# Two weight-sum steps and one transpose step reordered at the entry of a four-layer graph network's last layer

## The chip, the core and the metric

The kernel runs on one core of one Trainium2 chip. The metric is device time in microseconds (us), from the start to the end of one execution. PE is the matrix engine, DVE the vector engine, ACT the scalar engine, POOL the general engine (GpSimd), and SP the engine that issues nearly all transfers here.[...]

## What is computed

The input `x` is 128 graphs of 64 nodes with 256 features; `adj` is a 64 by 64 adjacency matrix. Four graph layers follow each other, each inside a residual connection and a layer norm:

```
x = _layernorm(x + _L0_gnn_ref(x, adj, ...))
x = _layernorm(x + _L1_gnn_ref(x, ..., adj, ...))
x = _layernorm(x + _L2_gnn_ref(x, adj, ...))
x = _layernorm(x + _L3_gnn_ref(x, adj, ...))
```

Only the passage into the last layer matters here:

```
h = relu(einsum('ts,bsh->bth', adj, x @ Wg0 + bg0))
h = relu(einsum('ts,bsh->bth', adj, h @ Wg1 + bg1))
for p in range(1, MAX_SKIP + 1):          # window lengths 1, 2, 3, 4
    wins = windows of p neighbouring rows of h
    last = last hidden state of an LSTM of length p over each window
    h = h with the last row of each window set to last
```

So the third layer's output is normed, goes through two graph convolutions, and then through four LSTMs with window lengths 1 to 4, each with its own input weights `Wih[p-1]` and recurrent weights `Whh[p-1]`.

## The kernel before

**Blocks.** The last layer works on 16 blocks of 8 graphs (512 rows). A block's way from the third layer's result to the LSTM's input is one generator, `gcn`. Its steps are: scale (ACT, L1294; of the first four blocks, which are still on the chip); two norm steps, each of which transposes half of the block on PE (L1312), adds the residual rows `x2r` (DVE, L1318), takes the statistics (DVE, L95 to L98), raises the variance to the power -1/2 (POOL, L86), scales (POOL, L100) and writes the half to DRAM (SP, L1323); the first sum over neighbours (PE, L1280) with its copy `hT` (DVE L1343, ACT L1344); the two halves of the first weights (PE L1350, DVE L1352, ACT L1354); the two halves of the second (PE L1362, DVE L1365); and the second sum over neighbours with the write of `H` (PE L1280, DVE L1373, ACT L1374). The residual rows come from DRAM by `load_x2` (SP, L1004); those of blocks 0 and 1 are fetched long before, those of block 2 when its generator is first called. PE's results go into banks called `g` (two) and `l` (six).

**LSTMs.** The generator `lstm` handles a pair of groups (four blocks). It starts once blocks 0 and 1 are through. Many of its products are formed by seven multiplications in place of eight, from sums and differences of the four parts of a weight matrix. These weight sums are made once, on POOL: `first_sums` (L1397, four operations 128x384) for the windows of length 1, and `Weights.sums` (L1229, four operations 128x512) twice for each of the lengths 2 to 4, once for the input weights (`wx`) and once for the recurrent ones (`wh`). Each is also written to DRAM, for later pairs: L1399 (0.75 MB), and L1232 (2 MB for `wx`, 1.75 MB for `wh`). `prepare` is the generator that loads a length's raw weights (L1218, 1 MB each), and then makes and writes one set of sums at each later call. The sums on the data, `column_sums`, are L1417 to L1420, also on POOL.

**Order.** `given(do)` ties the instructions that it records behind the ones recorded before, on PE, DVE, ACT and POOL, so on these engines the order is that of the program's text. SP's is not tied: it follows from the scheduler of the language. At the entry a list of block numbers says which block makes its next step, and `side` says which steps are put between the LSTM's units (`put(0, first[0], 3, 4)` puts the length-2 sums after units 3 and 4).

Before the change the entry is: `first_sums`, then the list of steps, then the LSTM's beginning, then a few more steps, then the length-2 loads.

Of the kernel before, what the change touches and what calls it, by code (L numbers as in the profile page):

```python
# [41 lines left out]
def kernel(ctx: ExitStack, tc: tile.TileContext, i, out):  # L42
# [67 lines left out]
    def given(do, *args, **more):  # L110
        traced = nc.cur_bb.bb.instructions
        first = len(traced)
        with ExitStack() as order:
            for e in latest.values():
                order.enter_context(tc.issue_after(e))
            r = do(*args, **more)  # L116
        for t in traced[first:]:
            if t.engine in (mybir.EngineType.PE, mybir.EngineType.DVE, mybir.EngineType.Activation,
                            mybir.EngineType.Pool):
                latest[t.engine] = t  # L120
        return r
# [8 lines left out]
    with ExitStack() as two:  # L130
# [630 lines left out]
        def hidden(q, m):  # L761
            return Z[q][:, m, :] if m < 2 else Aq(q)[:, (m - 2) * QT:(m - 1) * QT]
# [15 lines left out]
        def put(q, m, p_):  # L778
            nc.scalar.activation(hidden(q, m), p_, AF.Identity, bias=b1[:, m:m + 1])
            nc.vector.bn_stats(st1[:, m, q, :], hidden(q, m))  # L780
# [300 lines left out]
        def prepare(q):  # L1081
            terms[q] = []
            later = [(k, n) for k in range(M1) for n in range(2)]

            def one():
                k, n = later.pop(0)
                given(relu, q + 2 + n, k)
            for g in range(2):
                b = lambda k, n, g=g: hidden(q + n, 2 * g + k)
                a = lambda m, k, g=g: w2[:, 2 * g + k, m * P:(m + 1) * P]  # L1090
                T = sums_in_order(b)
                next(T)
                one()
                yield
                terms[q].append((a, [SW[1][:, n, g] for n in range(4)], b, next(T)))
                one()
                if g == 0:
                    one()
                yield
            one()  # L1100
            yield
            one()
            one()
# [792 lines left out]
    parts = [gcn(n // 2, n % 2, gbank if n % 2 == 0 else lbank, "hT" if n % 2 == 0 else "xs") for n in range(4)]  # L1896
    first = [prepare(weights_of[0, p]) for p in (2, 3)]
    for p in (2, 3):
        weights_of[0, p].room()
    given(first_sums)  # L1900
    for n in [0, 0, 0, 1, 1, 0, 1, 0, 0, 1, 2, 0, 0, 2, 1, 2, 1, 0, 3, 1, 1, 1]:
        given(next, parts[n])
    lstms = [lstm(k) for k in range(NP)]
    next(lstms[0])
    for n in [2, 3, 2, 3, 2]:
        given(next, parts[n])
    next(first[0])

# [7 lines left out]
    for u, order in enumerate([(3, 2, 2, 3, 3), (3, 3, 2, 3)]):  # L1918
        for n in order:
            put(0, parts[n], u)  # L1920
    put(0, first[0], 3, 4)
    put(0, first[1], 8, 13, 15)

    def gap(u):
# [80 lines left out]
```

## Time and profile before

| What | Value |
|---|---|
| Median of 3 runs | 2040.4 us (2037.68 to 2045.28) |
| Profiled execution: its time, and its span | 2039.12 us, 2037.3 us |
| PE busy | 1940.1 us, 95% of the span |
| DVE, ACT, POOL busy | 1248.0, 988.0, 880.0 us |
| PE's share of the chain that ended last | 73% |
| PE busy in 750 to 760 us | 7.13 of 10 us |
| PE busy in 830 to 840 and 850 to 860 us | 8.57 and 7.87 of 10 us |
| SP waiting for L1229 before L1232, 755 to 870 us | 5.6 us (`wx`), 8.3 us (`wh`) |

The span is what the trace covers; the execution's own time is 1.8 us more. The last layer begins near 760 us and fills the rest. In a timeline line the columns are: start, duration, engine, source line, operation, output and inputs, shape, count, and in brackets the engine's idle time before it with what ended it. A line with x2 or x4 merges that many instructions; its duration goes from the first's start to the last's end. SPq is SP issuing a transfer: the duration is that of the issue, not of the transfer. `A` is the block's room on the chip, `x_dram` a DRAM tensor, and `sums` the DRAM copies of weight sums.

### The profile page before, as it was taken

What the parts mean: (1) busy time and instruction counts of PE and PEld (TensorE: products, weight loads), DVE (VectorE), ACT (ScalarE), POOL (GpSimd) and SP (SyncE); (2) the same over time, 40 slices, a digit from 0 to 9 for tenths busy, and PEclk for the clock granted to TensorE, in tenths of its full rate; (3) what the DMA queues carried; (4) which work ended last, traced back from release to release, by engine and by line L of the source; (5) the groups of instructions that cost most, each with busy time, mean ns of one, the idle gap of its engine ahead of it and who ended that gap; (6) DMA issues with size and microseconds to landing.
All of it is one profiled execution on the core that took longest, in us unless ns stands there. A gap on an engine that the chain in (4) does not pass through costs nothing.

```text
span 2037.3 us, 31496 instructions
## 1 busy us (share of the span) xinstructions
PE 1940.1 (95%) x11447; PEld 1337.8 (66%) x11447; DVE 1248.0 (61%) x2763; ACT 988.0 (48%) x1892; POOL 880.0 (43%) x1017
## 2 busy tenths in 40 slices
PE   5999999999999999899999999999999999999996
PEld 4667777766554445477678577667577668578685
DVE  7456565565456555765557865557775557664566
ACT  2766666666345633644343644333544333543333
POOL 1123333333445544564645543435543445444264
PEclk8999999999999998999999999999999999999999
DMA  5344443332302025433243243133143032132022
GB/s 129 85 67 65 83 68 55 66 45 39 51 22 60 38 93 185 148 139 107 86 162 92 66 155 136 39 132 88 58 152 121 24 111 66 47 119 78 0 62 73
DMA packets 236539, 173.84 MB, mean 85 GB/s; under 512 B 150624, under 2 KB 213600, under 8 KB 233056
## 3 DMA queue, kind: packets, MB, share of 16 engines
q1 hardware_dynamic: 234528, 169.86, 29.5%
q8 instruction: 90, 1.47, 0.3%
q0 software_dynamic: 1024, 1.05, 0.2%
q10 hardware_dynamic: 832, 0.92, 0.1%
q14 instruction: 65, 0.53, 0.1%
HBM read 110.18 MB, written 61.60 MB: 84 GB/s over the span
## 4 chain that ended last, share of the span: by engine, by line
PE 73%; DVE 14%; ACT 5%; DMA 3%; issue 3%; POOL 2%; SPq 1%; DVEq 0%; POOLq 0%; ACTq 0%
PE l L1728 27%; PE l L1684 8%; PE pz L845 4%; PE l L1463 4%; PE m L253 3%; PE pz L774 3%; PE m L324 3%; PE e L352 2%; PE m L446 2%; PE g L1362 2%; PE m L327 2%; PE z L361 2%; PE g L1350 2%; PE pz L1043 2%; DVE cell L1642 1%
## 5 line engine op out<-in xcount | busy, mean ns | idle before, releaser
L1728 PE MATMUL l<-hs,wh 128*128 128x256 f32 (+1 forms) x896 | 276.0, 399 | 3.7 <-DVE hs L1592 3.1
L1728 PE MATMUL l<-xs,wx 128*128 128x256 f32 (+1 forms) x896 | 276.2, 399 | 2.9 <-DVE gate L1747 2.7
L1743 ACT ACTIVATE kept<-l 128x256 f32<-128x256 f32 (+1 forms) x224 | 88.8, 403 | 333.2 <-PE l L1728 331.8
L86 POOL TENSOR_TENSOR ln_rs<-ln_rs,mhalf 128x2 f32<-128x2 f32 (+2 forms) x98 | 85.5, 873 | 367.4 <-DVE ln_rs L98 366.9
L1728 PE MATMUL l<-H,wx 128*128 128x256 f32 (+1 forms) x672 | 210.5, 402 | 4.3 <-DVE gate L1756 3.4
L1728 PE MATMUL l<-hid,wh 128*128 128x256 f32 (+1 forms) x672 | 208.7, 399 | 0.0
L1728 PEld LDWEIGHTS l<-hs,wh 128*128 128x128 f32 x896 | 169.1, 190 | 47.1 <-DVE hs L1592 5.7
L1728 PEld LDWEIGHTS l<-xs,wx 128*128 128x128 f32 x896 | 168.9, 190 | 46.1 <-issue 2.8
L1761 ACT ACTIVATE gate<-gate,bias 128x512 f32<-128x512 f32 (+1 forms) x280 | 170.6, 657 | 40.7 <-DVE gate L1752 34.8
L1684 PE MATMUL l<-H,wx 128*128 128x256 f32 (+5 forms) x672 | 185.2, 431 | 4.9 <-DVE H L116 2.7
L363 ACT ACTIVATE u<-z 128x1024 f32<-128x1024 f32 x128 | 130.3, 1026 | 68.8 <-PE z L361 67.7
L1684 PEld LDWEIGHTS l<-H,wx 128*128 128x128 f32 x672 | 118.8, 190 | 65.5 <-issue 34.2
L1728 PEld LDWEIGHTS l<-H,wx 128*128 128x128 f32 x672 | 125.7, 190 | 42.6 <-DVE gate L1756 7.4
L1728 PEld LDWEIGHTS l<-hid,wh 128*128 128x128 f32 x672 | 127.2, 190 | 32.0 <-issue 2.9
L1751 POOL TENSOR_TENSOR gate<-gate,kept 128x256 f32<-128x256 f32 (+1 forms) x84 | 65.1, 775 | 144.9 <-DVE kept L1749 136.2
L335 DVE TENSOR_TENSOR qs<-m,qs 64x256 fp32r<-64x256 f32 x128 | 54.0, 422 | 106.3 <-ACT qs L334 104.4
L361 PE MATMUL z<-gath_r,qs 128*128 128x512 f32 x256 | 100.4, 480 | 9.3 <-ACT u L363 8.9
L1756 DVE TENSOR_TENSOR gate<-l,gate 128x256 f32<-128x256 f32 (+1 forms) x112 | 50.0, 446 | 88.4 <-POOL gate L1751 64.3
L1596 POOL TENSOR_TENSOR hs<-hid 128x256 f32<-128x256 f32 (+1 forms) x28 | 26.0, 929 | 170.1 <-DVE hid L1628 87.0
L1650 ACT ACTIVATE gate<-cell 128x512 f32<-128x512 f32 (+1 forms) x88 | 58.6, 666 | 83.6 <-DVE cell L1642 61.5
L1638 POOL TENSOR_TENSOR cell<-gate,cell 128x512 f32<-128x512 f32 (+1 forms) x56 | 75.4, 1367 | 28.4 <-ACT gate L1761 28.4
L1745 DVE TENSOR_TENSOR gate<-l,kept 128x256 f32<-128x256 f32 (+1 forms) x112 | 49.1, 438 | 59.7 <-ACT gate L1761 32.6
(380 smaller groups left out, 4097.6 us busy)
## 6 DMA issues: line engine op xcount, KB each, us to landing
wx<-sums SPq DMA_DIRECT2D x9, 2048.0 KB
wh<-sums SPq DMA_DIRECT2D x9, 1792.0 KB
way<-st SPq DMA_DIRECT2D x54, 256.0 KB
st<-way SPq DMA_DIRECT2D x216, 64.0 KB
xin<-in_x SPq DMA_DIRECT2D x16, 512.0 KB
ld<-table SPq DMA_DIRECT2D x16, 512.0 KB
x_dram<-y SPq DMA_DIRECT2D x16, 512.0 KB
x2r<-x_dram SPq DMA_DIRECT2D x32, 256.0 KB
```

The costliest lines, as they stand in the source:

```text
L86: nc.gpsimd.tensor_tensor(dst, dst, mhalf[:, :n], OP.pow)
L253: nc.tensor.matmul(p_, xT[:, k, c * P:(c + 1) * P], w0[:, k, :], start=k == 0, stop=k == KD - 1)
L361: nc.tensor.matmul(z[:, k, :], L1[q]["qs"][c][:, s, k * P:(k + 1) * P], gath_r, start=True, stop=True)
L363: nc.scalar.activation(u, z, AF.Relu)
L845: nc.tensor.matmul(self.bank[at], lhs, rhs, start=first and n == 0, stop=n == len(self.terms) - 1, skip_group_check=True)
L1463: nc.tensor.matmul(self.bank[at], lhs, rhs, start=new, stop=True, skip_group_check=True)
L1638: nc.gpsimd.tensor_tensor(c, t, c, OP.mult)
L1684: nc.tensor.matmul(b, w.raw[0][:, k, at, m, :], x, start=k == 0, stop=k == KD - 1)
L1728: nc.tensor.matmul(self.banks[j], lhs, rhs, start=src == 0, stop=src == 1)
L1743: nc.scalar.activation(self.keep(j), b, AF.Copy)
L1751: e.tensor_tensor(t[0][:, 1], t[0][:, 1], k[5], OP.add)
L1761: given(lambda: nc.scalar.activation(dst, dst, f, bias=b))
```

## The change

In the entry, `first_sums` moves from ahead of all steps to behind the norm steps of blocks 0 and 1 and block 0's first sum over neighbours. The second norm step of block 1 (its transposes on PE, its addition on DVE, its power and scaling on POOL) moves ahead of block 0's first sum over neighbours. The length-2 raw weights are loaded first of all, and the length-2 sums, with their writes to DRAM, move into the entry: those of `wx` ahead of block 2's first step, and those of `wh` after block 2's second norm step. Their former places, behind units 3 and 4 of the LSTM, go. No operation is added or dropped.

```diff
@@
     first = [prepare(weights_of[0, p]) for p in (2, 3)]
     for p in (2, 3):
         weights_of[0, p].room()
-    given(first_sums)
-    for n in [0, 0, 0, 1, 1, 0, 1, 0, 0, 1, 2, 0, 0, 2, 1, 2, 1, 0, 3, 1, 1, 1]:
-        given(next, parts[n])
+    next(first[0])
+    order = [0, 0, 0, 1, 1, 1, 0, first_sums, 0, 0, 1, first[0], 2, 0, 0, 2, 1, 2, first[0], 1, 0, 3, 1, 1, 1]
+    for n in order:
+        if n is first_sums:
+            given(n)
+        else:
+            given(next, parts[n] if isinstance(n, int) else n)
     lstms = [lstm(k) for k in range(NP)]
     next(lstms[0])
     for n in [2, 3, 2, 3, 2]:
         given(next, parts[n])
-    next(first[0])
@@
     for u, order in enumerate([(3, 2, 2, 3, 3), (3, 3, 2, 3)]):
         for n in order:
             put(0, parts[n], u)
-    put(0, first[0], 3, 4)
     put(0, first[1], 8, 13, 15)
```

As built, the order on the engines changes in this way. PE: block 1's last four transposes (L1312) come ahead of block 0's L1280. DVE: block 1's second L1318 and its statistics come ahead of block 0's L1343. POOL: the four norms of blocks 0 and 1, then L1397, then L1229 on `wx`, then block 2's two norms, then L1229 on `wh`, then L1417. SP: the two loads L1218, the eight writes L1323, L1399, L1232 for `wx`, then L1004 for blocks 2 and 3, two loads of later blocks (L1298), four L1323, L1004, and L1232 for `wh`. Before, SP had L1004 for blocks 2 and 3 directly after the first eight L1323, and both L1232 some 60 us later.

## The prediction

> **What bounds the kernel now.** I read the page first: PE is busy 95% of the span, 31,496 instructions, and the chain that ended last is mostly matmuls, so time can only be won where PE stands still or runs slowly. The change touches 757 to 866 us, so the rest comes from there. The windows of that stretch (columns: total, PE, PE weight load, DVE, ACT, POOL busy, then clock, DMA share, GB/s) show where PE is not full:
>
> ```profile
> 760.00:770.00 10.00, 5.47 (x78) 4.51 (x78) 6.59 (x25) 3.06 (x6) 8.09 (x11) 0.54 0.67 248
> 770.00:780.00 10.00, 10.00 (x96) 6.04 (x89) 5.21 (x12) 4.06 (x8) 2.94 (x6) 0.78 0.52 158
> 780.00:790.00 10.00, 9.65 (x99) 6.49 (x98) 7.26 (x20) 4.03 (x8) 3.59 (x6) 1.00 0.58 203
> 840.00:850.00 10.00, 8.22 (x20) 3.53 (x19) 7.86 (x15) 6.20 (x10) 7.47 (x7) 1.00 0.58 238
> ```
>
> Two places stand out: the entry into the last layer (PE half idle at half clock), and 840 to 850. The timeline of the entry says why:
>
> ```profile
> 761.54 1.96 POOL L1397 TENSOR_TENSOR wh<-wih 128x384 f32<-128x384 f32 x2 [1.98 <-PE g L1312]
> 763.44 0.17 DVE L85 TENSOR_SCALAR ln_rs<-ln_mv 128x2 f32<-128x2 f32 x1
> ...
> 764.66 0.99 POOL L1397 TENSOR_TENSOR wh<-wih,wh 128x384 f32<-128x384 f32 x1
> ...
> 765.61 0.71 POOL L86 TENSOR_TENSOR ln_rs<-ln_rs,mhalf 128x2 f32<-128x2 f32 x1
> ...
> 767.03 1.25 PE L1280 MATMUL g<-bdT,A 64*64 64x64 f32 x32 [3.47 <-POOL A L100]
> ...
> 770.20 0.69 DVE L1343 COPY hT<-g 128x512 f32<-128x512 f32 x1 [2.59 <-PE g L1280]
> ...
> 775.55 1.85 SPq L1004 DMA_DIRECT2D x2r<-x_dram  x4
> ...
> 781.79 0.68 DVE L1318 TENSOR_TENSOR x2r<-g,x2r 128x512 f32<-128x512 f32 x1
> ```
>
> The first norm is ready for POOL at 763.61 (763.44 + 0.17), but POOL works on `first_sums` until 765.65: 2.0 us in which the norm waits and PE behind it. The last two lines are the ones to remember: SP fetches block 2's residual rows `x2r` at 775.55, DVE uses them at 781.79. That is 6.2 us of lead, and nothing waits.
>
> For the second place, DVE and PE, and then SP's queue further on:
>
> ```profile
> 836.11 3.29 DVE L116 TENSOR_TENSOR H<-gate,cell 128x512 f32<-128x512 f32 x2
> 840.79 1.29 DVE L116 TENSOR_TENSOR H<-gate,wh 128x512 f32<-128x512 f32 x2 [0.20 <-ACT gate L116]
> ```
>
> ```profile
> 842.83 1.10 PE L1463 MATMUL l<-wx,wih 128*128 128x512 f32 x2 [1.78 <-DVE hs L116]
> 851.61 1.13 PE L1463 MATMUL l<-wx,wh 128*128 128x512 f32 x2 [0.81 <-DVE gate L116]
> ```
>
> ```profile
> 826.82 0.32 SPq L1265 DMA_DIRECT2D way<-st  x1
> 828.86 1.74 SPq L1267 DMA_DIRECT2D st<-way  x4
> ...
> 979.63 0.34 SPq L1232 DMA_DIRECT2D sums<-wx  x1
> 980.07 0.38 SPq L1265 DMA_DIRECT2D way<-st  x1
> 987.12 1.75 SPq L1267 DMA_DIRECT2D st<-way  x4
> ```
>
> The same pair of multiplications takes 3.29 us while POOL runs the length-2 sums (L1229, 834.66 to 840.53) and 1.29 us after them. And a 256 KB transfer (`way`) whose reader follows at once is read 2.04 us after its issue when alone (826.82 to 828.86), but 7.05 us after it when a 2 MB write of sums stands 0.44 us ahead of it on the queue (980.07 to 987.12). That last figure decides my forecast.
>
> [...] here `way`, whose input DVE had ready at 835.60 (834.89 + 0.71), was issued at 840.99, just after the sums' write at 840.56. [...] Before, PE ends at 757.1, the clock is 0.50 from 761, and 1.00 again from 774.5, after near-unbroken work since 767.03.
>
> **The change part by part.** The base is the profiled execution: span 2037.3, its run 2039.12, 1.3 below the median 2040.4.
>
> 1. *first_sums behind the four norms of blocks 0 and 1.* POOL starts the first norm at 763.65 and not 765.61, 1.96 earlier. The next bound is DVE: block 1's second norm now stands ahead of block 0's `hT` copy. DVE's norms start at 761.71, 763.59 and 765.66, 1.95 each; four end at about 769.6. So `hT` is copied at 769.6 and not 770.20: 0.6 won of 1.96, by itself.
>
> 2. *Block 1's second transposes earlier.* Four transposes (1.11 us, half clock) leave 770.08 and go into the gap of 763.5 to 767. They lie beside the hT wait, so they add nothing to the 0.6.
>
> 3. *The POOL queue.* Four norms at 1.87 (765.61 to 767.48) bounded by DVE's 1.95: the last power starts at 763.65 + 3 x 1.95 = 769.5 and its scaling ends at 771.4. Then `first_sums`, 4.1 us (761.54 to 765.65), to 775.5. Then the length-2 `wx` sums, four of 1.27 plus gaps, 5.2 us (5.65 and 5.87 before, beside two-input DVE work that is absent here), to 780.7.
>
> 4. *The SP queue, the part that costs.* The program's SP order is now: `wx` and `wh` loads, eight `x_dram` writes, the write of first_sums (0.75 MB), the write of the `wx` sums (2 MB), and only then block 2's `x2r`. The 2 MB write waits for POOL at 780.7; `x2r` is issued 0.44 later, at 781.2, in place of 775.55, behind 2 MB. By the `way` pair it lands 7.05 later: 788.2. DVE's addition, 781.79 before, comes at 788.3: **6.5 late**. Behind it on DVE's queue stand `xs` L1352 and block 2's second addition; PE's L1280 for block 0 needs both g banks, which these additions free, and started 3.6 after the addition (785.39 against 781.79). So PE stops at some 785 and goes on at 791.9. The 0.6 of part 1 is swallowed.
>
> 5. *The clock.* PE stands still for 6 to 7 us, more than the 3.9 us after which it was halved before (757.1 to 761). The work from 791.9 starts at half clock. Recovery took 7.5 us from 767.03 with gaps, [...] less the 1.2 us of small waits PE had in 785 to 798. I take 2.0 (bounds 0.5 and 3.5).
>
> 6. *Length-2 sums gone from 834 to 850.* The two multiplications come back from 3.29 to 1.29; the 1.78 stall at 842.83 hangs on the DVE work behind them: 1.7 won. POOL's add at 849.67 stood behind the `wh` sums (844.05 to 849.70) though its input was there at 847.2; the `x2r` addition at 847.15 took 1.43 and not 0.68. The 0.81 stall at 851.61 goes. The sum is 2.5; bounds 1 and the stalls at 842.83, 851.61, 854.00 and 859.92 together, 3.9. Next bound there is DVE's chain from 851. The new place of the `wh` sums, after block 2's second norm (some 794.6 to 800), is free: the column sums behind it began 5.2 us after that norm's scaling ended and now wait for `H`, which shifts by 8.5 as well.
>
> 7. *Writes of sums moved off SP at 835 to 850.* `way` and `st` go out 5 to 9 us earlier; DVE's addition of them at 860.98 followed at once on earlier DVE work, so nothing is won.
>
> Sum: +6.5 + 2.0 - 2.5 = **+6.0 us**, span 2043.3, run 2045.1, against the median **2046.4**, or 0.3%. From 798 to 833 PE has no idle time in which the delay could be lost.
>
> **Rivals.** *A, slightly faster:* `x2r` lands in some 2 us like a lone `way`, because reads pass the write. Then DVE is 781.2 + 2.0 = 783.2, 1.4 late, PE idles under 2 us and keeps its clock: +1.4 - 2.5 = -1.1, 2039.3; with no lateness at all, -0.6 - 2.5 = -3.1, 2037.3. For it: `x2r` is a read into SBUF, `way` a write to DRAM, and no run shows a read behind a write of sums with its reader waiting. Against: one queue carries both. It decides if landing takes under 3.5 us. *B, clearly slower:* the write moves at about 250 GB/s and not 400 (the trace shows 385 and 401 beside such writes, and 254 elsewhere), 8.4 and not 5.2 us: +3.2 on part 4, [...] relief only 1.5 (+1.0): +11.6, 2052. For it: 2 MB, then 256 KB pieces, on one queue. Against: the 7.05 is itself measured. *C, larger relief:* 3.9 in part 6 and 0.5 in part 5 give +3.1, 2043.5; inside my own range. That the edit does nothing is excluded by the program's order on POOL and SP.
>
> **How the numbers follow.** Forecast with C: 0.66, range 2042 to 2050. A: 0.21. B: 0.13. The range for 8 in 10 takes in half of A and most of B's near side: 2038 to 2052. About 0.5%, 10.2 us, is what a measurement of this kernel can tell from no change, so the forecast and A lie within it: faster 0.03 (no idle time of that size is at stake), same 0.85, slower 0.12 (B and the tail of the forecast).
>
> **What would show it.** Right: POOL's first power near 763.7; the SP issue of block 2's `x2r` near 781 behind L1232; DVE L1318 near 788 with a wait on that DMA; PE idle 5 to 7 us before L1280, then clock 0.50; L1229 gone from 834 to 850 and the 1.78 stall with it. Wrong: L1318 at 783 or earlier (A), or PE's stall under 3 us. If POOL finishes the `wx` sums later than 782, part 3 is mis-sized and all of it moves with it.

## The result, and the profile after

The changed kernel takes 2045.11 us (median of 20 runs, 2041.9 to 2050.1), the kernel before 2040.88 (20 runs, 2034.26 to 2045.28). The ratio is 1.0024, with a 95% interval of 1.0016 to 1.0033: **about 4.9 us slower** (3.3 to 6.7); the two medians differ by 4.2. The forecast was 2046.4 in a range of 2038 to 2052.

Where the time lies can't be read off the spans alone. The profiled execution of the changed kernel has a span of 2048.3 us, 11 more than before. But its last layer (DVE's memset L1247, the first instruction of it) begins at 765.58 and not 760.12, and nothing that the change moves runs ahead of that. The ten profiles of this study have that memset anywhere between 755.06 and 765.58. So below, "layer time" is the time since that memset. The first block of the page, of the changed kernel:

```profile
span 2048.3 us, 31502 instructions
PE 1949.3 (95%) x11447; PEld 1343.2 (66%) x11447; DVE 1244.7 (61%) x2763; ACT 988.2 (48%) x1892; POOL 877.7 (43%) x1017
```

PE is busy for 9.2 us more than before (1949.3 against 1940.1) with no product added: products at half clock count longer (16 instructions of L1362 take 3.72 us from 782.62, at a clock of 1.00, and 6.14 us from 799.31, where the clock is 0.50 up to 804). Not all of this is the change's: 4.8 us of it lie ahead of the memset (707.69 against 702.90), and 4.4 in the first 111 us of the layer (98.63, against 94.20 in the first 106 us before). The timeline of the entry, changed kernel, which answers to the one shown of before:

```profile
768.89 0.70 POOL L86 TENSOR_TENSOR ln_rs<-ln_rs,mhalf 128x2 f32<-128x2 f32 x1 [3.86 <-DVE ln_rs L98]
...
774.78 0.68 DVE L1343 COPY hT<-g 128x512 f32<-128x512 f32 x1
...
780.80 5.20 POOL L1229 TENSOR_TENSOR wx<-wx 128x512 f32<-128x512 f32 x4
...
786.02 0.32 SPq L1232 DMA_DIRECT2D sums<-wx  x1
...
786.43 3.94 SPq L1004 DMA_DIRECT2D x2r<-x_dram  x4
...
794.19 0.69 DVE L1318 TENSOR_TENSOR x2r<-g,x2r 128x512 f32<-128x512 f32 x1 [7.12 <-DMA x2r<-x_dram]
...
794.94 1.97 PE L1280 MATMUL g<-bdT,st 64*64 64x64 f32 x32 [4.28 <-DVE x2r L1318]
...
797.40 1.97 PE L1280 MATMUL g<-bdT,st 64*64 64x64 f32 x32 [0.49 <-DVE x2r L1318]
```

Read the third line to the sixth as one sentence: POOL forms the `wx` sums until 786.00; SP, which held their write for it for 4.8 us, sends that write and at once the four reads of block 2's and 3's rows; the rows are there 7.8 us later, and DVE, idle for 7.12 us, adds them. In layer time the addition comes at 28.61 (794.19 - 765.58) instead of 21.67 (781.79 - 760.12). PE waits 4.28 us for it. The chain of waits that ended last now goes through this transfer (start, duration):

```profile
786.43 7.64 DMA x2r<-x_dram
```

The windows of the changed kernel behind it (columns as before; the clock is the third number from the end):

```profile
792.00:794.00 2.00, 0.00 (x0) 0.00 (x0) 0.00 (x0) 0.00 (x0) 0.00 (x0) 1.00 0.64 245
794.00:796.00 2.00, 1.06 (x20) 1.06 (x22) 1.74 (x7) 0.00 (x0) 0.00 (x0) 0.50 1.03 394
...
802.00:804.00 2.00, 2.00 (x6) 1.61 (x5) 0.69 (x1) 0.64 (x2) 1.92 (x2) 0.50 0.83 255
804.00:806.00 2.00, 2.00 (x38) 1.43 (x37) 0.52 (x1) 0.00 (x0) 1.73 (x2) 0.94 0.02 7
```

All engines but the transfers stand still in the first line, and PE then works at half clock for ten microseconds. Against this stands the second place, where the length-2 sums have gone. DVE's pair of multiplications, from DVE's timeline of the changed kernel, took 3.29 us before:

```profile
850.73 1.27 DVE L116 TENSOR_TENSOR H<-gate,cell 128x512 f32<-128x512 f32 x2
```

PE's stalls of 1.78, 0.81 and 0.42 us there (before: 842.83, 851.61, 854.00) are gone, and the 0.90 at 859.92 is down to 0.61.

Three marks in layer time give the balance: block 2's first addition (DVE L1318), the LSTM's first product (PE L1531), and the third group of L1684 behind it. After that the two kernels run alike: what is left of the span is 1171.56 us before and 1171.83 in the changed kernel (1170.29 to 1171.83 in all ten profiles). A few tenths of a microsecond in these columns belong to the execution and not to the kernel: block 0's first addition, which no edit moves, comes at 1.33 to 1.39 in eight of the ten, at 1.59 before and at 1.97 in e1.

| Kernel | Block 2's addition | First L1531 | Third L1684 | Third L1684 against before | Ratio of the times, 95% interval |
|---|---|---|---|---|---|
| before | 21.67 | 38.01 | 105.62 | | |
| changed | 28.61 | 47.18 | 110.89 | +5.27 | 1.0024 (1.0016 to 1.0033) |
| e2_first_sums_only | 21.49 | 37.83 | 105.45 | -0.17 | 0.9992 (0.9983 to 1.0001) |
| e1_rows_first | 21.20 | 37.54 | 101.24 | -4.38 | 0.9977 (0.9966 to 0.9987) |
| e8_wh_sums_left | 21.44 | 37.77 | 103.40 | -2.22 | 0.9986 (0.9980 to 0.9993) |
| e3_small_write_first | 24.43 | 41.68 | 105.40 | -0.22 | 1.0002 (0.9991 to 1.0014) |
| e6_write_twice | 33.61 | 51.50 | 115.22 | +9.60 | 1.0038 (1.0024 to 1.0052) |
| e4_filled_gap | 29.80 | 46.14 | 109.86 | +4.24 | 1.0011 (1.0002 to 1.0020) |
| e5_old_transposes | 19.11 | 37.09 | 100.79 | -4.83 | 0.9972 (0.9957 to 0.9987) |
| e7_clock_kept | 17.62 | 34.79 | 98.50 | -7.12 | 0.9965 (0.9952 to 0.9979) |

For the changed kernel: +6.94 at the addition, another +2.23 up to L1531, then -3.90, is +5.27. One thousandth of the ratio is 2.04 us, so the trace's balance and the ratio agree in every row but one (e4, below). The columns of times come from one execution each.

### The profile page after: what moved, and what is told of

Read it like the earlier page. It is cut to its first block, busy times and chain, and to the rows that moved or that the text cites. A ratio compares the mean times of both kernels' runs of the same rounds, so it can differ in the third digit from the quotient of the medians.

```text
span 2048.3 us, 31502 instructions
## 1 busy us (share of the span) xinstructions
PE 1949.3 (95%) x11447; PEld 1343.2 (66%) x11447; DVE 1244.7 (61%) x2763; ACT 988.2 (48%) x1892; POOL 877.7 (43%) x1017
## 4 chain that ended last, share of the span: by engine, by line
PE 73%; DVE 15%; ACT 4%; DMA 3%; issue 2%; POOL 2%; SPq 0%; DVEq 0%; POOLq 0%; ACTq 0%
PE l L1728 27%; PE l L1684 7%; PE l L1463 5%; PE pz L845 4%; PE pz L774 3%; PE e L352 3%; PE m L324 3%; PE m L253 3%; PE m L446 2%; PE z L361 2%; PE m L327 2%; PE g L1362 2%; PE pz L1043 2%; PE g L1350 2%; DVE cell L1642 1%
## 5 line engine op out<-in xcount | busy, mean ns | idle before, releaser
L1684 PE MATMUL l<-H,wx 128*128 128x256 f32 (+5 forms) x672 | 185.0, 431 | 4.6 <-DVE H L116 2.4
L1684 PEld LDWEIGHTS l<-H,wx 128*128 128x128 f32 x672 | 118.8, 190 | 65.0 <-issue 34.2
```

Of the source, the lines that this page charges most:

```text
L1684: nc.tensor.matmul(b, w.raw[0][:, k, at, m, :], x, start=k == 0, stop=k == KD - 1)
```

## The experiments

The theory: the whole loss is one chain, SP's wait for POOL, then the 2 MB write ahead of the rows, then PE's idle gap and its clock; the removal of the length-2 sums from 834 to 850 us is a gain by itself. The rivals: the loss lies in the new places of the sums or transposes themselves; the rows do not wait for the bytes ahead of them, only for SP; the half clock costs nothing because the entry is bound elsewhere.

**The rows fetched first.** The change in full, but `x2r` of blocks 2 and 3 is fetched ahead of `first_sums`:

```diff
     for n in order:
         if n is first_sums:
+            early.update({q: load_x2(q) for q in (2, 3)})
             given(n)
```

> The changed kernel with one edit: the residual rows of blocks 2 and 3 are fetched ahead of first_sums, so on SP they no longer stand behind the two writes of sums. Theory Q (queue: the changed kernel loses its time because block 2's rows are issued after the wait for the wx sums and land behind a 2 MB write): DVE's L1318 for block 2 waits for no transfer, PE has no gap of over 1 us before block 0's second L1280, the clock stays at 1.00 there, and what is left is the gain at the entry (0.6) and the relief at units 3 and 4 (3.9 in the changed kernel's trace): 2040.9 - 4.5 = 2036.4, 0.998 of the kernel before. Theory P (POOL: the sums' 5.2 us in the entry delay block 2's norms, or disturb DVE there): no better than the changed kernel, 2044 to 2046.

Measured: 2035.11 us, ratio 0.9977. Its timeline:

```profile
770.57 1.86 SPq L1004 DMA_DIRECT2D x2r<-x_dram  x4
...
779.39 0.32 SPq L1232 DMA_DIRECT2D sums<-wx  x1
779.47 0.68 DVE L1318 TENSOR_TENSOR x2r<-g,x2r 128x512 f32<-128x512 f32 x1
```

No bracket stands behind DVE's addition: it waits for nothing. Only SP's order differs from the changed kernel, and the addition, the gap and the second half clock are all back to what they were. SP's order costs the change some 10 us (0.9977 against 1.0024; 110.89 - 101.24 = 9.65 in the traces), which is more than its whole loss; the rest of the change is a gain of 4 to 5 us.

**The first half of the change alone.** The length-2 sums go back to units 3 and 4, and their loads behind the list:

```diff
-    next(first[0])
-    order = [0, 0, 0, 1, 1, 1, 0, first_sums, 0, 0, 1, first[0], 2, 0, 0, 2, 1, 2, first[0], 1, 0, 3, 1, 1, 1]
+    order = [0, 0, 0, 1, 1, 1, 0, first_sums, 0, 0, 1, 2, 0, 0, 2, 1, 2, 1, 0, 3, 1, 1, 1]
...
+    next(first[0])
...
+    put(0, first[0], 3, 4)
```

> The first half of the change alone: first_sums behind the norms of blocks 0 and 1, block 1's second norm step ahead of block 0's first sum; the length-2 loads and sums stay where they were before the change. Theory Q: block 0's hT copy 0.6 earlier than in the kernel before, no stall for block 2's rows, the L1229 stalls at units 3 and 4 as before: 2040.3, between 2039 and 2041. Theory P, or any theory that puts the loss on the new order of norms: slower than the kernel before, by up to the 4 us of the changed kernel.

Measured: 2040.05 us, 0.9992 (0.9983 to 1.0001): no difference that can be told, and -0.17 in the trace. The copy `hT` came 0.87 us earlier in layer time, yet block 2's addition only 0.18. The next product shows where the rest went. PE's timeline, of this kernel and of the kernel before:

```profile
771.54 6.12 PE L1350 MATMUL g<-hT,wg 128*128 128x512 f32 x8 [2.27 <-issue]
```

```profile
771.00 5.41 PE L1350 MATMUL g<-hT,wg 128*128 128x512 f32 x8
```

Before, block 1's transposes ran ahead of this product and kept PE at work (L1312, 1.11 us from 770.08); now PE stands still for 2.27 us. The product starts earlier (9.99 against 10.88 in layer time) and lasts longer, because the clock, 0.50 there in both, is set free later: about 14.9 against 14.4, from the mean clock of the two windows in which it turns (0.88 at 776 to 778, and 0.88 at 774 to 776). What the norm gained, the clock took. Why it was set free later is not shown. The moved transposes are one candidate and the chance of the execution is the other: with the same order on PE the clock came free at about 13.6 in e1_rows_first (0.81 in 770 to 775) and at 14.8 in the changed kernel (0.66 in 780.0 to 780.5).

**Only the `wx` sums in the entry.** This is e1_rows_first with the `wh` sums left behind unit 4:

```diff
-    order = [0, 0, 0, 1, 1, 1, 0, first_sums, 0, 0, 1, first[0], 2, 0, 0, 2, 1, 2, first[0], 1, 0, 3, 1, 1, 1]
+    order = [0, 0, 0, 1, 1, 1, 0, first_sums, 0, 0, 1, first[0], 2, 0, 0, 2, 1, 2, 1, 0, 3, 1, 1, 1]
...
+    put(0, first[0], 4)
```

> The version of e1_rows_first, with only the wx sums of length 2 in the entry; the wh sums go back behind unit 4 of the LSTM, where they ran at 844 to 850 us before. This splits the relief of part 6, which was 3.9 us and not 2.5, between its two halves. By the forecast's reasoning the multiplications that took 3.29 us ran beside the wx sums and the stall of 1.78 us hangs on them; the wh sums held only DVE's addition (1.43 against 0.68 us) and the stalls of 0.81 and 0.42. So 1.8 to 2.1 us of the relief stay, and the stalls of 0.81 and 0.42 us come back: the third L1684 of the unit comes about 1.9 us later from the start of the layer than in e1_rows_first, 2037.0 us. Rival: the two stretches depend on each other, because without the wx sums DVE is early enough at 844 us to ride out the second stretch; then nearly all the relief stays, 2035.1 to 2035.8.

Measured: 0.9986 (2033.74 us; the kernel before took 2036.35 on this chip, so the times of this run are not set beside the others, only the ratio). The third L1684 is at 103.40, 2.16 later than in e1. From L1531 to the third L1684 it is 67.61 us before, 65.63 here, 63.70 in e1: the two halves are worth 1.98 and 1.93 us, and they add up. Timelines of POOL, DVE and PE of this kernel:

```profile
836.77 5.66 POOL L1229 TENSOR_TENSOR wh<-wh 128x512 f32<-128x512 f32 x4
```

```profile
830.84 1.27 DVE L116 TENSOR_TENSOR H<-gate,cell 128x512 f32<-128x512 f32 x2
...
839.86 1.44 DVE L1318 TENSOR_TENSOR x2r<-st,x2r 128x512 f32<-128x512 f32 x1
...
842.41 1.27 DVE L98 TENSOR_SCALAR ln_rs<-ln_mv 128x2 f32<-128x2 f32 x1
```

```profile
844.33 1.13 PE L1463 MATMUL l<-wx,wh 128*128 128x512 f32 x2 [0.82 <-DVE gate L116]
846.73 1.12 PE L1463 MATMUL l<-wx,wih 128*128 128x512 f32 x2 [0.41 <-DVE wx L116]
```

The pair at 830.84 is short and its stall gone; the slow addition and the stalls of 0.8 and 0.4 are back, as expected. The third DVE line was in the profile before too, and I had passed over it: L98, a small operation on 128 by 2 numbers, takes 1.27 us. POOL's own add (L116, 842.39 to 843.65), pushed back by the `wh` sums, runs beside it. Without the sums L98 takes 0.16 us, here in e1_rows_first:

```profile
844.59 0.16 DVE L98 TENSOR_SCALAR ln_rs<-ln_mv 128x2 f32<-128x2 f32 x1
```

**A small write ahead of the rows in place of the large one.** SP still waits for POOL, but only 128 KB of the 2 MB stand ahead of the rows:

```diff
-            nc.sync.dma_start(d, t)
+            if self.p == 2 and n == 0:
+                nc.sync.dma_start(d[:, 7, :DH // 2], t[:, 7, :DH // 2])
+                early.update({q: load_x2(q) for q in (2, 3)})
+                nc.sync.dma_start(d[:, 7, DH // 2:], t[:, 7, DH // 2:])
+                nc.sync.dma_start(d[:, :7], t[:, :7])
+            else:
+                nc.sync.dma_start(d, t)
```

> The changed kernel with the 2 MB write of the wx sums cut in three: 128 KB first, which waits for POOL as the whole did; then the fetch of the rows of blocks 2 and 3; then the remaining 1.9 MB. So SP's wait stays and the large write ahead of the rows goes. Theory Q splits the lateness: the wait costs what a lone transfer issued at 5 us later costs (rows in use 1.5 to 2.5 us later than before the change, PE's gap under 3 us, no fall of the clock), the write ahead costs the remaining 5 us: 2040.9 + 2.0 - 3.9 = 2039.0. Rival W (the wait on SP alone is what costs): rows as late as in the changed kernel, near 2045.

Measured: 2041.72 us, 1.0002: level with before, and 2.7 slower than expected. Timeline (later lines carry numbers 6 higher, so L1324 is L1318) and windows:

```profile
779.11 0.32 SPq L1233 DMA_DIRECT2D sums<-wx  x1
...
779.53 1.82 SPq L1004 DMA_DIRECT2D x2r<-x_dram  x4
...
783.06 0.69 DVE L1324 TENSOR_TENSOR x2r<-g,x2r 128x512 f32<-128x512 f32 x1 [2.82 <-DMA x2r<-x_dram]
...
786.27 1.20 PE L1286 MATMUL g<-bdT,st 64*64 64x64 f32 x62 [2.14 <-DVE x2r L1324]
```

```profile
786.00:788.00 2.00, 1.73 (x64) 1.52 (x64) 1.93 (x8) 0.28 (x1) 1.43 (x3) 0.81 1.00 422
788.00:790.00 2.00, 1.82 (x5) 1.02 (x4) 1.02 (x2) 1.88 (x4) 1.90 (x4) 0.50 0.88 339
```

The rows land 3.53 us after their issue (783.06 - 779.53), against 7.76 behind 2 MB. So of the lateness of 6.94, 2.76 belongs to SP's wait for POOL together with the 128 KB, and 4.18 to the rest of the 2 MB. The price behind it was under-estimated: a gap of only 2.14 us was followed by the half clock all the same, and the lateness of 2.76 became 3.67 at L1531.

**The 2 MB written twice.** The added write goes to a DRAM tile that nobody reads:

```diff
             d = dram.tile(list(t.shape), F32, name=f"sums{self.p}_{n}")
+            if self.p == 2 and n == 0:
+                nc.sync.dma_start(dram.tile(list(t.shape), F32, name="again"), t)
             nc.sync.dma_start(d, t)
```

> The changed kernel, with the 2 MB write of the wx sums issued twice, the added one to a DRAM tile that nobody reads, both ahead of block 2's residual rows on SP. If the rows wait for the bytes written ahead of them on the queue, the landing of the rows (7.76 us after issue with one write) grows by a further 4 to 5 us, to about 12.5, L1318 of block 2 comes as much later, PE's gap grows from some 4.8 to about 9.5 us, and the time is 2050 us (2049 to 2051) against 2045.1. Rival: the rows are late only because they are issued behind a wait on POOL, or the writes share the engines' bandwidth so that the rows' own descriptors advance beside them: then the second write adds under 1.5 us, 2045 to 2046.5.

Measured: 2048.61 us, 1.0038. Timeline (numbers 2 higher):

```profile
783.73 0.32 SPq L1233 DMA_DIRECT2D again<-wx  x1
...
784.10 0.42 SPq L1234 DMA_DIRECT2D sums<-wx  x1
...
784.62 4.77 SPq L1004 DMA_DIRECT2D x2r<-x_dram  x4
...
796.91 0.69 DVE L1320 TENSOR_TENSOR x2r<-g,x2r 128x512 f32<-128x512 f32 x1 [12.01 <-DMA x2r<-x_dram]
```

The rows land 12.29 us after their issue: 3.53, 7.76, 12.29 for 0.125, 2 and 4 MB ahead of them, or 4.2 and 4.5 us for each step of about 2 MB. (Behind 2 MB a second execution, that of e4 below, had 8.83, so these steps are good to about 1 us.) The lateness grows with the bytes ahead, and the rival, that the rows pass the write, is out. Block 2's addition comes 5.00 later than in the changed kernel, L1531 4.32, the time some 3 us by the ratios (1.0038 against 1.0024), a little less than expected. Between the addition and L1531 0.68 us are won back (17.89 against 18.57), and that is the clock: PE's L1362 takes 5.46 us here and 6.14 in the changed kernel. The clock fell to half at about 791.9 (0.98 in 790 to 792, 0.50 in 792 to 794), 5.7 us ahead of PE's restart at 797.65. By an estimate from L1362's 5.46 us, against 3.72 at full clock, it was free at 805.5. So only 7.9 us of it fell behind the restart, against 9.3 in the changed kernel.

**The gap filled.** Products that feed nothing, put between the last product ahead of PE's gap (block 1's L1350) and block 0's second L1280, keep PE at work:

```diff
+    def idle_products():
+        b = lbank([QT])
+        for _ in range(10):
+            nc.tensor.matmul(b, wih1[:, 0, :P], wih1[:, 0, :QT], start=True, stop=True)
+
-    order = [0, 0, 0, 1, 1, 1, 0, first_sums, 0, 0, 1, first[0], 2, 0, 0, 2, 1, 2, first[0], 1, 0, 3, 1, 1, 1]
+    order = [0, 0, 0, 1, 1, 1, 0, first_sums, 0, 0, 1, first[0], 2, 0, 0, 2, 1, 2, first[0], 1, idle_products, 0, 3, 1, 1, 1]
```

> The changed kernel with ten products of 128x512 added on PE, into a bank that nobody reads, in the gap in which PE waits for block 2's rows (4.3 us at full clock, the gap's length). It adds work and keeps all waits. Theory Q with the clock as its second term: the clock stays at 1.00 after the gap, block 1's L1362 takes 3.7 us and not 6.1, and some 2.2 us come back: 2043.0. Rival (the clock's fall is covered by waits for DVE): no change, 2045, or slower by what the added products overrun the gap.

Measured: 2041.81 us, 1.0011. PE's timeline, and a window behind the gap:

```profile
782.22 8.75 PE L1904 MATMUL l<-wih 128*128 128x512 f32 x20
```

```profile
790.00:792.00 2.00, 2.00 (x68) 1.17 (x66) 1.93 (x8) 0.37 (x1) 1.43 (x3) 1.00 0.32 115
```

Ten products are twenty instructions, twice what I had reckoned, and so they fill the whole gap; L1280 follows at 790.89, 3.74 us after the addition (3.60 before), so they cost next to nothing themselves. The clock stays at 1.00. Block 2's addition is 8.13 late in this execution (the rows took 8.83 us to land), and L1531 is 8.13 late: with the clock kept, lateness passes on one to one. So the further 2.23 us of the changed kernel are the net price of its half clock. Alone the half clock may cost somewhat more, since the changed kernel starts half of L1280 0.75 us after the addition, while the filling products hold it back as long as before. Why the rows landed 1.1 us later here is not settled. That this row's +4.24 lies above what the ratio allows (0.4 to 4.1 us) is no contradiction: behind the third L1684 this execution is 1.27 us shorter than the one before, and from the memset to the end of the span it is +2.97.

**Two steps further.** Both edits are shown against e1_rows_first. The first puts block 1's second norm step back behind block 0's first sum, where it was before the change:

```diff
-    order = [0, 0, 0, 1, 1, 1, 0, first_sums, 0, 0, 1, first[0], 2, 0, 0, 2, 1, 2, first[0], 1, 0, 3, 1, 1, 1]
+    order = [0, 0, 0, 1, 1, 0, 1, first_sums, 0, 0, 1, first[0], 2, 0, 0, 2, 1, 2, first[0], 1, 0, 3, 1, 1, 1]
```

> The version of e1_rows_first (residual rows of blocks 2 and 3 fetched ahead of the writes of sums), with block 1's second norm step put back behind block 0's first sum over neighbours, where it stood before. By my part 1 the second norm step ahead of hT let only 0.6 of the 1.96 us through, because DVE's statistics of block 1 then stand ahead of the copy hT. Without it, hT is copied about 1.2 us earlier from the start of the layer than in e1_rows_first, and block 1's four transposes (1.11 us at half clock) come back into PE's work of 767 to 772: a gain of some 0.9 us at most at block 0's first weights, 2034.2 us against e1's 2035.1. Rival: the end of the entry is set by block 1's second half (its norm is now later by the same amount), then the time is that of e1_rows_first or up to 1 us more, 2035 to 2036, and the first product of the second weights does not come earlier.

Measured: 2035.09 us, 0.9972, against 0.9977 of e1: the times can't tell them apart. In the trace `hT` comes 2.07 us earlier than before in layer time (8.01 against 10.08), the whole of the 1.96 that POOL had cost, and block 2's first addition 2.56 earlier; but the third L1684 is only 0.45 earlier than in e1, less than the 0.63 by which e1's execution was late at block 0's first addition. So of this step's gain nothing is seen there. Block 2's norm now meets the `wx` sums (POOL and DVE of its timeline):

```profile
775.60 5.19 POOL L1229 TENSOR_TENSOR wx<-wx 128x512 f32<-128x512 f32 x4
...
779.57 1.25 DVE L98 TENSOR_SCALAR ln_rs<-ln_mv 128x2 f32<-128x2 f32 x1
```

Again the small L98 takes 1.25 us, ending with the sums, and block 2's second addition comes 3.56 us after the first and not 2.47.

Then the same with idle products in the two gaps of the entry:

```diff
+    def idle_products(n):
+        b = lbank([QT])
+        for _ in range(n):
+            nc.tensor.matmul(b, wih1[:, 0, :P], wih1[:, 0, :QT], start=True, stop=True)
+
+    given(idle_products, 4)
...
-    order = [0, 0, 0, 1, 1, 0, 1, first_sums, 0, 0, 1, first[0], 2, 0, 0, 2, 1, 2, first[0], 1, 0, 3, 1, 1, 1]
+    order = [0, 0, 0, 1, 1, idle_products, 0, 1, first_sums, 0, 0, 1, first[0], 2, 0, 0, 2, 1, 2, first[0], 1, 0, 3, 1, 1, 1]
     for n in order:
-        if n is first_sums:
+        if n is idle_products:
+            given(n, 2)
+        elif n is first_sums:
```

> The version of e5_old_transposes with idle products on PE that feed nothing: four of 128x512 ahead of the layer's first matmul and two ahead of block 0's first sum over neighbours, in gaps in which PE stood still. Before and in e1, PE runs at half clock from 761 to about 774 us. If the half clock costs time there, the clock stays at 1.00, and the matmuls of 763 to 774 (some 8 us of PE at half clock, of which about half stand on the way to block 0's first weights) give 2 us: 2032.2 us against e5. Rival: the path of the entry is POOL and DVE's norms, so only L1280 and L1350 behind hT gain, 0.5 to 1 us; or the products overrun the gaps, and nothing is won or up to 1.5 us lost.

Measured: 2033.56 us, 0.9965 (0.9952 to 0.9979), the fastest of all; the clock is 1.00 throughout the entry. PE's timeline (numbers 6 higher, so L1356 is L1350):

```profile
766.77 3.67 PE L1356 MATMUL g<-hT,wg 128*128 128x512 f32 x8 [0.26 <-ACT hT L1350]
```

The product that took 5.41 us before takes 3.67. In the trace the third L1684 is 2.29 earlier than in e5, as expected; the intervals of the two ratios overlap, so by the times alone this step is not shown.

## Why the forecast came out right, point by point

*Parts 1 and 2.* POOL's first power was forecast at 763.65 and came at layer time 3.31, which is 763.43 on the clock of the profile before. `hT` came 0.88 us earlier, 0.25 of it because the layer's first addition did (1.34 against 1.59); 0.6 was forecast, with DVE's statistics of block 1 as the next bound. The bound is shown by e5: with them out of the way, 2.07 arrive. What I had not seen is that by itself (e2) nearly nothing of it reaches block 2, because block 0's product then stays longer at half clock. The transposes, booked as free, had also kept PE at work; whether that is the reason is not shown.

*Part 3.* The `wx` sums were to end at 780.7; they ended at 786.00 - 5.46 = 780.54.

*Part 4.* Lateness 6.5 forecast, 6.94 measured. The landing, 7.05 by the pair of `way`, was 7.76. That the bytes ahead make it long is what the 3.53, 7.76 and 12.29 us behind 0.125, 2 and 4 MB show. Wrong was the detail that PE would stop for 6 to 7 us because L1280 needs both banks: half of the products started 0.75 us after the first addition (794.94 against 794.19), so the standstill was 4.28, then 0.49.

*Part 5.* 2.0 forecast, 2.23 measured, and e4 shows that it is the clock. That the sizes agree is partly luck. The gap was 4.28 us and not 6 to 7, though that was enough; the half clock was to last at most the 7.5 us of the profile before and lasted 10.2. The forecast's lower bound of 0.5 rested on an estimate of mine that no run here shows. By my estimate PE worked through 8.8 us of the half clock (794.94 to 804.24 less the wait of 0.49; the clock is 0.50 in the windows of 794 to 804), a loss of 4.4 us. Most of what was made up was not in the forecast's small waits (1.2 us there; the windows of the profile before give 0.87 in 784 to 798): PE took up L1280 0.75 us after the addition and not 3.60, 2.85 us sooner.

*Part 6* is the term that was mis-sized: 2.5 forecast, 3.90 measured (67.61 - 63.71). The `wx` half was nearly right (1.7 for the stall at 842.83; 1.98 by e8). The `wh` half was put at 0.8, the one stall of 0.81, and was 1.93: also the 0.42 behind it, part of the 0.90 at 859.92 and some idle time too short to be listed hang on it. L98 was on no list of mine: I had looked only at DVE's large additions and multiplications beside POOL's work. It took 1.27 us (e8) and 1.25 (e5) beside it, against 0.16 without it (e1); why so small an operation takes longer there is not shown. The upper bound of 3.9 was met, by a sum of stalls of which the last only shrank.

*Part 7.* Nothing was booked for the writes moved off SP; no run separates it from part 6.

Together: 6.94 + 2.23 - 3.90 = +5.27 in place of +6.5 + 2.0 - 2.5 = +6.0. Rival A needed a landing under 3.5 us: out, at 7.76. Rival B's larger lateness did not come; the 1.4 us of its +11.6 for a longer half clock was my estimate, not shown. Rival C, the larger relief, came in part: its relief exactly, its small clock term not. The total came nearer than its worst term because 0.44 and 0.23 us more in parts 4 and 5 offset half of the larger relief.

## What to carry to other kernels

When a step is moved, follow every transfer that it issues into the queue's order: here a write held for POOL, with 2 MB of its own, was put ahead of a 256 KB read that somebody waits for, and one line that fetches the rows first turns +4.9 us into -4.7. Price a lateness as a sum of three: what the issuer waits, what the bytes ahead take, and the slow clock after the gap (here 2.76 us with the first 128 KB, 4.18 and 2.23). Work on POOL that lengthens DVE's operations beside it (here 3.29 us against 1.27) is worth moving even if POOL has time, and the small operations count too (1.27 against 0.16).

## What was not expected of the hardware

A gap of 2.14 us was followed by the fall of PE's clock to half (e3), where a gap under 3 us had been expected to leave it: PE had worked without a break up to 784.13, started again at 786.27 with 64x64 products, and the clock fell in 786 to 788. The half clock itself lasted 10.2 us in the changed kernel (from 794 to 804.24, by the 0.94 of the window 804 to 806) and 3.4 us in e3 (from 787.25, by the 0.81 of 786 to 788, to 790.66, by the 0.83 of 790 to 792). In e6, behind a gap of 9.18 us, it lasted some 13.6 us (from 791.9 to 805.5, the end by estimate). So the cost did not grow evenly with the gap in these three runs: behind PE's restart lay 3.4, 9.3 and 7.9 us of half clock for gaps of 2.14, 4.28 and 9.18 us. How much work keeps the clock up is not shown.
